# A graph layer and an 8-bit feed-forward layer on one core: where the 8-bit scale's factor is multiplied in, and the order of four steps around a maximum over all rows

## The chip, the cores and the metric

The kernel runs on one core of one Trainium2 chip. The metric is the device time of one execution in microseconds (us), as the median of several runs. Engines are named as the profile names them: PE is TensorE (PEld its weight load), DVE is VectorE, ACT is ScalarE, POOL is GpSimd, SP is SyncE, which here only issues transfers.

## What is computed

x is a 384 x 1024 matrix. A graph attention layer is added to it, then a feed-forward layer:

```python
x = x + gnn(layernorm(x))          # 16 heads, mask from 6528 edges
x = x + ffn(layernorm(x))

def act_fake_quant(x, clip):
    scale = sigmoid(clip) * max(abs(x)) / 127          # one number for the whole matrix
    return clip(round(x / scale), -128, 127) * scale

def ffn(x):                                            # w_*: quantised in the same way, one scale per row
    xq = act_fake_quant(x, clip_x)
    h = act_fake_quant(silu(xq @ w_gate.T) * (xq @ w_up.T), clip_down)    # 352 columns
    return h @ w_down.T
```

The two scales of act_fake_quant are what matters here. Each needs the largest absolute value of a whole matrix, so nothing of that matrix can be rounded before all of it is known.

## The kernel before

Rows are worked on in three tiles of 128 (t = 0, 1, 2), columns in blocks of 128 or halves of 512. The first 320 us compute the graph layer: projections (L189), scores, weights and products per pair of heads. The order on PE, SP and POOL is written out by hand for the whole kernel, and from L737 on that of DVE and ACT as well, so every engine works in the order of the program text, and an instruction that waits holds everything behind it on its engine. The 8-bit weights are quantised early. They lie in wgT, wuT and wdT, and their scales in w_scale and wd_scale.

The end of the kernel is what the change touches:

- *Last projection and residual* (L799 to L822). For each tile, matmuls (L814) go to PSUM, and `residual` (L746) adds x, takes the largest value (`hi`) along, makes the mean and variance statistics (L753) and the smallest value (`lo`, L754). Tile 2 is cut into groups of 512, 256, 128 and 128 columns, so that little is left to do after the last matmul.
- *`normalise`* (L756). It makes the mean and variance, and `far` (L770), the largest distance of a row from its mean, from `above` and `below`. The square root is on ACT (L764), and its reciprocal with one correction step (L773 to L779) gives `rstd`. `row_max` (L783) is far x rstd, taken together with the maximum of the earlier tiles: the largest absolute value that the row will have after normalisation, known without reading the row. Tiles 0 and 1 are normalised on ACT (L793, L794). Tile 2 is normalised on DVE, in two halves of 512 columns (L796).
- *Turning* (`turn`, L849). PE transposes the normalised tile into PSUM, eight 128 x 128 blocks (L855). Between the turns stand 14 or 17 transposes of the identity (`keep_busy`, L857, L861) that compute nothing.
- *The first scale* (L869). `all_max` (L127) spreads the column of row maxima over the partitions with one transpose (L129) and reduces it (L131), which gives the same largest value in every partition. `act_scale` (L835) multiplies it with sigmoid(clip) / 127 (L838), which is the scale sx, and takes the reciprocal rx (L840). sx goes to POOL, which makes the factors of the gate and up products (`gu_scale`, L873).
- *Conversion* (L881 to L886). There are six pieces of 128 x 512: three tiles by two halves of the columns. ACT multiplies those of tiles 0 and 1 with rx and writes int8 (L883), DVE those of tile 2 (L884). DVE casts all six from int8 to bf16 (L886).
- *Gate and up* (L888 to L911). Four column groups of 16 matmuls each (L895). Of the first 16, the first eight need the first half of the columns (three casts), the others the second half. ACT takes the sigmoid (L901), DVE makes the products (L903, L906) and the largest absolute value of each partition (L909), in a column of `hmx` for each group.
- *The second scale* (L918 to L922). 17 idle transposes, then DVE reduces hmx to one column (L920), and the same all_max and act_scale give sh and rh. h is converted (L929, L931) and cast (L934), multiplied with w_down (L943), scaled (L947), and added to x on POOL (L951, three pieces) and DVE (L955, three pieces). Each piece is then stored.

The factor sigmoid(clip) comes from L482, at about 31 us.

Of the kernel before, what the change touches and what calls it, by code (L numbers as in the profile page):

```python
# [23 lines left out]
F32 = mybir.dt.float32  # L24
# [3 lines left out]
AF = mybir.ActivationFunctionType  # L28
ALU = mybir.AluOpType
# [3 lines left out]
P = 128  # L33
# [28 lines left out]
def gnn_ffn_kernel(ctx: ExitStack, tc: tile.TileContext, a: dict, out: bass.AP):  # L62
# [74 lines left out]
    mask = ffn.tile([P, NT, N], F32)  # L137
    nc.gpsimd.memset(mask, NO_EDGE)
    sig = ffn.tile([P, 2], F32)

    ident_b = const.tile([P, P], BF16)
    later = ph1.tile([P, GROUP * P], F32, name="later", bufs=1)
# [94 lines left out]
    def run(steps):  # L237
        for _ in steps:
            pass
# [6 lines left out]
    with ph1_stack:  # L246
# [37 lines left out]
        def normalise(t, between=None):  # L284
            xn = rows_p.tile([P, F], F32, name="row")
            for j in range(2):
                hs = slice(j * 512, (j + 1) * 512)
                nc.vector.tensor_scalar(
                    xn[:, hs], x[:, t, hs], mv1[:, t, 0:1], rstd1[:, t : t + 1], op0=ALU.subtract, op1=ALU.mult
                )  # L290
            for g in range(2):
                pt = ps_tp.tile([P, 4, P], F32, name="tp")
                for j in range(4):
                    c = 4 * g + j
                    nc.tensor.transpose(pt[:, j, :], xn[:, c * P : (c + 1) * P], ident)
                nc.scalar.copy(xnT[:, 4 * g : 4 * g + 4, t * P : (t + 1) * P], pt)
                if g == 0 and between:
                    between()
# [156 lines left out]
        for i, (name, o) in enumerate(todo[:-1]):  # L455
            (wa, wb), sums = wq_next, sums_next
            right, dst, cols = work[name]

            if name == "wq" and o == FIRST:
                aside = tables()  # L460
            elif name == "wiq" and o == KC - 2:
                aside = k_steps
            else:
                aside = islice(groups, GROUP + 1)
            wq_next = [load_w(todo[i + 1][0], todo[i + 1][1] + j) for j in range(2)]
            sums_next, steps = left_sums(*wq_next, turned if todo[i + 1][0] == "wik" else ph1)
            if name == "wv" and o == KC - 4:
                q_right, q_steps = right_sums(qT, ph1, "right")
                work["wiq"] = (q_right, q2, bias_of(3))
            if name == "wv" and o >= KC - 4:  # L470
                steps = in_turn(steps, islice(q_steps, 4))
            if name == "wiq" and o == KC - 4:
                k_right, k_steps = right_sums(kT, turned, "k_right")
                steps = in_turn(steps, islice(k_steps, 4))
            aside = in_turn(aside, steps)
            run(project2(
                wa, wb, sums, right, dst[:, o], dst[:, o + 1], cols[:, o : o + 1], cols[:, o + 1 : o + 2], ps_p, "p",
                lambda: next(aside, None),
            ))
            run(aside)  # L480
            if i == 0:
                nc.scalar.activation(sig, clip, AF.Sigmoid)  # L482
        run(groups)


# [58 lines left out]
    with ExitStack() as ph:  # L544
# [211 lines left out]
        def normalise(t, last, st, hi, lo):  # L756

            mv = small.tile([P, 2], F32, name="mv2")
            nc.vector.bn_aggr(mv, st.rearrange("p a b -> p (a b)"))
            mean = mv[:, 0:1]  # L760
            var = small.tile([P, 1], F32, name="var2")
            nc.vector.tensor_scalar(var, mv[:, 1:2], EPS, None, op0=ALU.add)
            s0 = small.tile([P, 1], F32, name="s2")
            nc.scalar.activation(s0, var, AF.Sqrt)  # L764
            above = small.tile([P, 1], F32, name="above")
            nc.vector.tensor_scalar(above, hi[:, last : last + 1], hi[:, 0:1], mean, op0=ALU.max, op1=ALU.subtract)
            below = small.tile([P, 1], F32, name="below")
            nc.vector.tensor_scalar(below, lo[:, last : last + 1], lo[:, 0:1], mean, op0=ALU.min, op1=ALU.subtract)
            far = small.tile([P, 1], F32, name="far")
            nc.vector.tensor_scalar(far, below, -1.0, above, op0=ALU.mult, op1=ALU.max)  # L770

            r0 = small.tile([P, 1], F32, name="r2")
            nc.vector.reciprocal(r0, s0)  # L773
            vr = small.tile([P, 1], F32, name="vr2")
            nc.vector.tensor_scalar(vr, r0, var, r0, op0=ALU.mult, op1=ALU.mult)
            nw = small.tile([P, 1], F32, name="nw2")
            nc.vector.tensor_scalar(nw, vr, -0.5, 1.5, op0=ALU.mult, op1=ALU.add)
            rstd = small.tile([P, 1], F32, name="rstd2")
            nc.vector.tensor_mul(rstd, nw, r0)  # L779
            if t == 0:  # L780
                nc.vector.tensor_mul(row_max[:, 0:1], far, rstd)
            else:
                nc.vector.tensor_scalar(  # L783
                    row_max[:, t : t + 1], far, rstd, row_max[:, t - 1 : t], op0=ALU.mult, op1=ALU.max
                )
            if t < NT - 1:

                minus = small.tile([P, 1], F32, name="minus")
                nc.vector.tensor_scalar(minus, mean, -1.0, None, op0=ALU.mult)
            for g in range(2):  # L790
                gs = slice(g * 512, (g + 1) * 512)
                if t < NT - 1:
                    nc.scalar.activation(xn[:, t, gs], x[:, t, gs], AF.Identity, bias=minus)  # L793
                    nc.scalar.activation(xn[:, t, gs], xn[:, t, gs], AF.Copy, scale=rstd)  # L794
                else:
                    nc.vector.tensor_scalar(xn[:, t, gs], x[:, t, gs], mean, rstd, op0=ALU.subtract, op1=ALU.mult)  # L796


        for t in range(NT):  # L799
            if t < NT - 1:  # L800
                groups, part = [(0, 512), (512, 512)], 512
            else:
                groups, part = [(0, 512), (512, 256), (768, 128), (896, 128)], 128
            st = small.tile([P, F // part, 6], F32, name=f"st2_{part}")
            hi = small.tile([P, 4], F32, name="hi")
            lo = small.tile([P, 4], F32, name="lo")
            for g, (c0, width) in enumerate(groups):
                pm = open_groups.get((t, g)) if t < NT - 1 else None
                ks = [NP - 1]
                if pm is None:  # L810
                    pool, name = (ps_mm, "mm") if g < 2 else (ps_sc, "sc")
                    pm, ks = pool.tile([P, 512], F32, name=name), range(KC)
                for k in ks:
                    nc.tensor.matmul(  # L814
                        pm[:, :width], outT[:, k, t * P : (t + 1) * P], wo[k][:, c0 : c0 + width],
                        start=(k == 0), stop=(k == KC - 1),
                    )
                residual(t, g, c0, width, part, pm, st, hi, lo)
                if 0 < g < len(groups) - 1:
                    nc.vector.tensor_tensor(hi[:, 0:1], hi[:, 0:1], hi[:, g : g + 1], op=ALU.max)  # L820
                    nc.vector.tensor_tensor(lo[:, 0:1], lo[:, 0:1], lo[:, g : g + 1], op=ALU.min)
            normalise(t, len(groups) - 1, st, hi, lo)  # L822
        run(prep)


    with ExitStack() as ph:
# [5 lines left out]
        hmx = small.tile([P, 4], F32, name="hmx")  # L832
        nc.gpsimd.memset(hmx, 0.0)

        def act_scale(mx, which):  # L835

            s = small.tile([P, 1], F32, name=f"as{which}")
            nc.vector.tensor_scalar(s, mx, sig[:, which : which + 1], 1.0 / QMAX, op0=ALU.mult, op1=ALU.mult)  # L838
            r = small.tile([P, 1], F32, name=f"ar{which}")
            nc.vector.reciprocal(r, s)  # L840
            return s, r

# [21 lines left out]

        idle = small.tile([P, 1], F32, name="idle")
        nc.scalar.activation(idle, clip[:, 0:1], AF.Sigmoid)
        sx, rx = act_scale(all_max(row_max[:, NT - 1 : NT], pt[:, :P]), 0)  # L869
        turn(2)  # L870
        keep_busy(14, ps_x, "x")
        gu_scale = small.tile([P, 2, 3], F32, name="gu_scale")
# [8 lines left out]
        for g in range(2):  # L881
            for t in range(2):
                nc.scalar.activation(part(x8, t, g), xnT[t][g], AF.Copy, scale=rx)  # L883
            nc.vector.tensor_scalar(part(x8, 2, g), xnT[2][g], rx, None, op0=ALU.mult)  # L884
            for t in (0, 2, 1):
                nc.vector.tensor_copy(part(xqT, t, g), part(x8, t, g))  # L886

        for col, ic, c0, width in ((0, 0, 0, N), (1, 1, 0, N), (2, 2, 0, N // 2), (3, 2, N // 2, N // 2)):  # L888
# [28 lines left out]
            nc.scalar.copy(wd_scale_b[:, g * 512 : (g + 1) * 512], pt.rearrange("p a b -> p (a b)"))  # L917
        keep_busy(17, ps_x, "x")  # L918
        mx = small.tile([P, 1], F32, name="hmax")
        nc.vector.tensor_reduce(mx, hmx, axis=AX.X, op=ALU.max)  # L920
        pt = ps_tp.tile([P, P], F32, name="tp")
        sh, rh = act_scale(all_max(mx, pt), 1)  # L922

        h8 = ff.tile([P, 3, N], I8, name="h8", bufs=1)
        hq = ff.tile([P, 3, N], BF16, name="hq", bufs=1)
# [78 lines left out]
```

## Time and profile before

| what | value |
|---|---|
| median of 3 runs | 375.97 us (375.29 to 376.2) |
| the profiled execution's own time | 376.68 us |
| its span, first to last instruction | 374.9 us |
| mean granted PE clock | 0.994 |
| PE, DVE, ACT, POOL busy | 96%, 69%, 30%, 19% of the span |
| last matmul of the graph layer ends (L814) | 343.77 us |
| gate and up matmuls start (L895) | 350.28 us |
| conversion of h starts (L929) | 362.31 us |

All places in the text are us from the start of the span. The profile's page gives busy times by engine and the chain of work that ended last: followed back from the last instruction, at each step to what released it. The timeline lists instructions in order with start, length, engine, line and shape, and behind them in brackets how long the engine had idled and for whom. Lengths of neighbours on one engine overlap a little, since a step starts before the one ahead has left the pipeline. So the distance from start to start is what a step costs the engine, and start plus length is when its result is there. Each result that another instruction waits for is announced by a semaphore. A wait costs some hundredths of a us, even on the same engine.

### The profile page before, as it was taken

How to read it: one execution, taken by the hardware profiler on the slowest of the kernel's cores; microseconds unless marked ns; L12 is line 12 of the kernel's file. 1: busy time of each engine (PE TensorE's matmuls, PEld its weight loads, DVE VectorE, ACT ScalarE, POOL GpSimd, SP SyncE). 2: the span in 40 equal slices, each digit the busy share in tenths (PEclk: the TensorE clock that was granted, in tenths of full speed). 3: DMA queues.
4: the chain of work that ended last, by engine and by line, in shares of the span. 5: the costliest groups of instructions: out<-in, count | busy, mean ns of one | idle time of the engine just before them, and what ended most of it. 6: DMA issues, size and time to landing. Idle time of an engine off the chain costs nothing.

```text
span 374.9 us, 5872 instructions
## 1 busy us (share of the span) xinstructions
PE 358.8 (96%) x2113; PEld 298.9 (80%) x2113; DVE 260.2 (69%) x788; ACT 112.8 (30%) x264; POOL 72.1 (19%) x81
## 2 busy tenths in 40 slices
PE   8999999999999999799999999999999999999981
PEld 7899999999999999698877878686866545449660
DVE  5868888878889985998487457717492521199785
ACT  2152000100000000123672546446444523034330
POOL 6110254455444544210000000000000000000003
PEclk9999999999999999999999999999999999999997
DMA  8995433343333357148070040040294000000004
GB/s 236 393 376 213 150 114 112 116 133 114 112 112 115 112 170 247 57 119 289 21 231 32 19 129 23 18 171 1 101 375 132 31 0 2 0 0 3 1 0 168
DMA packets 17805, 44.50 MB, mean 119 GB/s; under 512 B 3263, under 2 KB 8401, under 8 KB 17393
## 3 DMA queue, kind: packets, MB, share of 16 engines
q1 hardware_dynamic: 15104, 39.46, 31.1%
q0 software_dynamic: 2672, 4.68, 4.2%
q8 instruction: 16, 0.26, 0.3%
q14 instruction: 13, 0.10, 0.1%
HBM read 41.91 MB, written 2.21 MB: 118 GB/s over the span
## 4 chain that ended last, share of the span: by engine, by line
PE 76%; DVE 12%; DMA 6%; ACT 3%; issue 1%; SPq 0%; DVEq 0%; ACTq 0%
PE p L189 34%; PE mm L580 7%; PE mm L189 6%; PE sc L641 4%; PE tp L633 4%; PE mm L651 3%; PE sc L651 3%; PE mm L814 3%; PE sc L603 3%; PE mm L303 3%; DMA row<-in_L_ffn_w_gate_dram 2%; DMA row<-in_L_ffn_w_down_dram 2%; DMA wt<-in_wik_dram 2%; PE sc L814 1%; DVE s L609 1%; DVE wmx L496 1%
## 5 line engine op out<-in xcount | busy, mean ns | idle before, releaser
L425 POOL DMA_INDIRECT mask_d<-value,place x51 | 56.9, 1115 | 66.3 <-DVE place L422 50.8
L189 PE MATMUL p<-actT,wt 128*128 128x192 f32 x360 | 65.9, 326 | 0.5 <-DVE actT L200 0.5
L189 PEld LDWEIGHTS p<-actT,wt 128*128 128x128 f32 x360 | 59.6, 190 | 0.8 <-DVE actT L200 0.8
L580 PE MATMUL mm<-wt,actT 128*128 128x256 f32 x192 | 46.1, 384 | 0.0
L580 PEld LDWEIGHTS mm<-wt,actT 128*128 128x128 f32 x192 | 34.8, 190 | 7.8 <-issue 2.2
L613 ACT ACTIVATE e<-s,mn 128x384 f32<-128x384 f32 x48 | 29.0, 605 | 26.4 <-DVE mn L609 26.4
L609 DVE CUSTOM_DVE_ANT_0 s<-sc,mask 128x384 f32<-128x384 f32 x48 | 24.5, 551 | 13.0 <-PE sc L603 12.8
L189 PE MATMUL p<-x_right,s 128*128 128x192 f32 x176 | 32.2, 326 | 0.0
L189 PE MATMUL p<-x_right,wt 128*128 128x192 f32 x176 | 32.2, 326 | 0.0
L831 POOL MEMSET hT<- 128x384 f32 x1 | 0.4, 418 | 156.9 <-PE sc L641 156.9
L189 PEld LDWEIGHTS p<-x_right,s 128*128 128x128 f32 x176 | 29.2, 190 | 0.0
L189 PEld LDWEIGHTS p<-x_right,wt 128*128 128x128 f32 x176 | 29.2, 190 | 0.0
L635 ACT COPY eTs<-tp 128x384 f32<-128x384 f32 x48 | 20.5, 478 | 25.3 <-PE tp L633 25.3
L412 DVE SCALAR_TENSOR_TENSOR junk<-key_b,key,later 128x384 f32<-128x384 f32 (+3 forms) x51 | 27.5, 539 | 0.0
L203 ACT COPY actT<-p 128x192 f32<-128x192 f32 x15 | 4.8, 319 | 66.9 <-PE p L189 66.9
L200 DVE SCALAR_TENSOR_TENSOR actT<-p,bias,actT 128x192 f32<-128x192 f32 x45 | 18.7, 415 | 8.5 <-PE p L189 6.6
L213 ACT ACTIVATE actT<-p,bias 128x192 f32<-128x192 f32 x15 | 6.3, 422 | 52.7 <-PE p L189 52.7
L633 PEld LDWEIGHTS tp<-ident,e 128*128 128x128 f32 x144 | 17.1, 140 | 4.9 <-issue 2.4
L633 PE MATMUL tp<-ident,e 128*128 128x128 f32 x144 | 19.7, 273 | 0.3 <-ACT eTs L635 0.3
L603 PE MATMUL sc<-k,actT 64*128 64x384 f32 x96 | 19.9, 518 | 0.0
L189 PE MATMUL mm<-actT,wt 128*128 128x192 f32 x96 | 18.9, 329 | 0.0
L496 DVE TENSOR_REDUCE wmx<-row 128x1 f32<-128x352 f32 (+2 forms) x14 | 11.4, 815 | 9.5 <-DMA row<-in_L_ffn_w_down_dram 6.4
(215 smaller groups left out, 596.3 us busy)
## 6 DMA issues: line engine op xcount, KB each, us to landing
wt<-in_wq_dram SPq DMA_DIRECT2D x8, 512.0 KB, 11.1
wt<-in_wk_dram SPq DMA_DIRECT2D x8, 512.0 KB, 4.3
wt<-in_wv_dram SPq DMA_DIRECT2D x8, 512.0 KB, 4.3
wt<-in_wiq_dram SPq DMA_DIRECT2D x8, 512.0 KB, 4.0
wt<-in_wik_dram SPq DMA_DIRECT2D x8, 512.0 KB, 4.5
wt<-in_wiv_dram SPq DMA_DIRECT2D x8, 512.0 KB, 5.3
wt<-in_wo_dram SPq DMA_DIRECT2D x8, 512.0 KB, 7.5
actT<-in_x_dram SPq DMA_DIRECT2D x6, 512.0 KB, 4.4
```

The costliest lines, as they stand in the source:

```text
L189: nc.tensor.matmul(z, left[:, k * P : (k + 1) * P], r[:, k, :], start=(k == 0), stop=(k == HK - 1))
L200: nc.vector.scalar_tensor_tensor(dst, z, b, with_, op0=ALU.add, op1=ALU.add)
L412: nc.vector.scalar_tensor_tensor(junk[:, :left], keys[:, (c - k0) * P : (c - k0) * P + left], key[:, c : c + 1], later[:, :left], op0=ALU. ...
L425: ins = nc.gpsimd.indirect_dma_start(out=mask_d, out_offset=bass.IndirectOffsetOnAxis(ap=place[:, c : c + 1], axis=0), in_=value[:, c : c ...
L496: nc.vector.tensor_reduce(mx[:rows], wn[:rows, :n], axis=AX.X, op=ALU.max, apply_absolute_value=True)
L580: nc.tensor.matmul(pm, vT[:, k, t * P : (t + 1) * P], wt[k // HK][:, k0 : k0 + 256], start=(k == 0), stop=(k == KC - 1),)
L603: nc.tensor.matmul(ps[t, h], q2[hs, t * P : (t + 1) * P], k2[hs, :], start=True, stop=True)
L609: nc.vector.tensor_tensor_reduce(s, ps[t, h], mask[:, t, :], -SCALE, 3.0e38, op0=ALU.add, op1=ALU.min, accum_out=mn[h][:, t : t + 1],)
L613: nc.scalar.activation(e[h][:, t, :], s, AF.Exp, bias=mn[h][:, t : t + 1], scale=-1.0, accum_out=sm[h][:, t : t + 1],)
L633: nc.tensor.transpose(pt[:, t * P : (t + 1) * P], e[h][:, t, m * P : (m + 1) * P], ident)
L635: nc.scalar.copy(eT[h][m], pt)
L651: nc.tensor.matmul(pm, outT[:, k, t * P : (t + 1) * P], wo[k][:, gs], start=(k == 0), stop=(k == KC - 1))
```

## The change

sigmoid(clip) / 127 is no longer multiplied onto the maximum over all partitions, but onto what goes into it. A new tile `per_max` holds the factor: column 0 for the first scale, columns 1 to 4 for the second. ACT makes it behind L482. In `normalise` the old `far` is now called `size`, and `far` is size x per_max, in all three tiles. For the second scale, the reduction of hmx becomes a multiplication with a maximum in one DVE instruction, which gives the column by an accumulator. What all_max returns is then the scale itself, and only the reciprocal is left to do.

The two halves of tile 2's normalisation leave `normalise`: the first stands ahead of the reduction of all_max on DVE, the second behind the reciprocal. On PE nothing is moved: the transposes of tile 2 still stand behind that of all_max, four for each half, and 14 idle ones follow.

Of the six conversions the last (tile 2, second half) goes from DVE to ACT, where it is the fifth. The casts of the first half now begin with tile 2, those of the second half end with it. In the built program the order on PE, POOL and SP is as it was; ACT has three instructions more, DVE one more: three more `far`, one accumulator read, less the two multiplications of act_scale and the one conversion.

```diff
+    per_max = ffn.tile([P, 5], F32)
...
                 nc.scalar.activation(sig, clip, AF.Sigmoid)
+                nc.scalar.activation(per_max[:, 0:1], sig[:, 0:1], AF.Copy, scale=1.0 / QMAX)
+                nc.scalar.activation(
+                    per_max[:, 1:5], sig[:, 1:2].to_broadcast([P, 4]), AF.Copy, scale=1.0 / QMAX
+                )
...
+            size = small.tile([P, 1], F32, name="size")
+            nc.vector.tensor_scalar(size, below, -1.0, above, op0=ALU.mult, op1=ALU.max)
             far = small.tile([P, 1], F32, name="far")
-            nc.vector.tensor_scalar(far, below, -1.0, above, op0=ALU.mult, op1=ALU.max)
+            nc.vector.tensor_mul(far, size, per_max[:, 0:1])
...
-                else:
-                    nc.vector.tensor_scalar(xn[:, t, gs], x[:, t, gs], mean, rstd, op0=ALU.subtract, op1=ALU.mult)
+            return mean, rstd
...
-        def act_scale(mx, which):
-
-            s = small.tile([P, 1], F32, name=f"as{which}")
-            nc.vector.tensor_scalar(s, mx, sig[:, which : which + 1], 1.0 / QMAX, op0=ALU.mult, op1=ALU.mult)
-            r = small.tile([P, 1], F32, name=f"ar{which}")
-            nc.vector.reciprocal(r, s)
-            return s, r
+        def last_tile(g):
+            gs = slice(g * 512, (g + 1) * 512)
+            t = NT - 1
+            nc.vector.tensor_scalar(xn[:, t, gs], x[:, t, gs], mean, rstd, op0=ALU.subtract, op1=ALU.mult)
...
-        sx, rx = act_scale(all_max(row_max[:, NT - 1 : NT], pt[:, :P]), 0)
+        last_tile(0)
+        sx = all_max(row_max[:, NT - 1 : NT], pt[:, :P])
+        rx = small.tile([P, 1], F32, name="ar0")
+        nc.vector.reciprocal(rx, sx)
+        last_tile(1)
         turn(2)
...
-            nc.vector.tensor_scalar(part(x8, 2, g), xnT[2][g], rx, None, op0=ALU.mult)
-            for t in (0, 2, 1):
+            if g == 0:
+                nc.vector.tensor_scalar(part(x8, 2, g), xnT[2][g], rx, None, op0=ALU.mult)
+            else:
+                nc.scalar.activation(part(x8, 2, g), xnT[2][g], AF.Copy, scale=rx)
+            for t in ((2, 0, 1), (0, 1, 2))[g]:
                 nc.vector.tensor_copy(part(xqT, t, g), part(x8, t, g))
...
-        nc.vector.tensor_reduce(mx, hmx, axis=AX.X, op=ALU.max)
+        scaled = small.tile([P, 4], F32, name="hscaled")
+        nc.vector.tensor_tensor_reduce(
+            scaled, hmx, per_max[:, 1:5], 1.0, -3.0e38, op0=ALU.mult, op1=ALU.max, accum_out=mx
+        )
...
-        sh, rh = act_scale(all_max(mx, pt), 1)
+        sh = all_max(mx, pt)
+        rh = small.tile([P, 1], F32, name="ar1")
+        nc.vector.reciprocal(rh, sh)
```

More of the change, by code (lines that the diff above doesn't have):

```diff
@@ L789, in normalise @@
                 nc.vector.tensor_scalar(minus, mean, -1.0, None, op0=ALU.mult)
-            for g in range(2):
-                gs = slice(g * 512, (g + 1) * 512)
-                if t < NT - 1:
+                for g in range(2):
+                    gs = slice(g * 512, (g + 1) * 512)
                     nc.scalar.activation(xn[:, t, gs], x[:, t, gs], AF.Identity, bias=minus)
                     nc.scalar.activation(xn[:, t, gs], xn[:, t, gs], AF.Copy, scale=rstd)
-                else:
-                    nc.vector.tensor_scalar(xn[:, t, gs], x[:, t, gs], mean, rstd, op0=ALU.subtract, op1=ALU.mult)
+            return mean, rstd
         for t in range(NT):
@@ L821, in gnn_ffn_kernel @@
                     nc.vector.tensor_tensor(lo[:, 0:1], lo[:, 0:1], lo[:, g : g + 1], op=ALU.min)
-            normalise(t, len(groups) - 1, st, hi, lo)
+            mean, rstd = normalise(t, len(groups) - 1, st, hi, lo)
         run(prep)
@@ L833, in gnn_ffn_kernel @@
         nc.gpsimd.memset(hmx, 0.0)
-        def act_scale(mx, which):
-            s = small.tile([P, 1], F32, name=f"as{which}")
-            nc.vector.tensor_scalar(s, mx, sig[:, which : which + 1], 1.0 / QMAX, op0=ALU.mult, op1=ALU.mult)
-            r = small.tile([P, 1], F32, name=f"ar{which}")
-            nc.vector.reciprocal(r, s)
-            return s, r
+        def last_tile(g):
+            gs = slice(g * 512, (g + 1) * 512)
+            t = NT - 1
+            nc.vector.tensor_scalar(xn[:, t, gs], x[:, t, gs], mean, rstd, op0=ALU.subtract, op1=ALU.mult)
         pt = ps_x.tile([P, 512], F32, name="x")
```

## The prediction

> **What bounds the kernel now.** I first read the page's busy shares and its chain that ended last. TensorE is busy for 96% of the span and carries 76% of the chain, so anything that only lightens VectorE in the first 320 us moves nothing.
>
> ```profile
> PE 76%; DVE 12%; DMA 6%; ACT 3%; issue 1%; SPq 0%; DVEq 0%; ACTq 0%
> ```
>
> Part of VectorE's 12% lies at the end, where one number (the largest value of all rows) must be known before anything can be rounded to 8 bits. The chain in order of time (start, us, what) shows that piece: row maximum, first normalised half, eight transposes of the last tile, conversion to int8, casts, matmuls.
>
> ```profile
> 345.47 0.21 DVE far L770
> 345.69 0.08 DVE r L773
> ...
> 346.76 0.46 DVE actT L796
> ...
> 347.27 1.12 PE mm L855 x8
> ...
> 348.42 0.75 DVE x L884
> 349.17 1.06 DVE xqT L886 x3
> 350.23 0.66 DVE x L884
> 350.89 1.01 DVE xqT L886 x3
> ...
> 351.94 0.32 PE mm L895
> ```
>
> The timeline (start, us, engine, line) of the same stretch corrects one step of it.
>
> ```profile
> 346.87 0.27 PE L129 MATMUL x<-ident,row_max 128*128 128x128 f32 x1
> ...
> 347.58 0.28 DVE L131 TENSOR_REDUCE allmax<-x 128x1 f32<-128x128 f32 x1
> 347.90 0.21 DVE L838 TENSOR_SCALAR as<-allmax,sig 128x1 f32<-128x1 f32 x1
> 348.15 0.16 DVE L840 RECIPROCAL ar<-as 128x1 f32<-128x1 f32 x1
> 348.21 1.69 PE L861 MATMUL x<-ident 128*128 128x128 f32 x14
> 348.22 0.32 POOL L873 TENSOR_SCALAR gu_scale<-w_scale,as 128x6 f32<-128x6 f32 x1 [27.44 <-DVE as L838]
> 348.41 0.69 ACT L883 ACTIVATE x<-tp,ar 128x512 int8<-128x512 f32 x1 [1.58 <-PE mm L855]
> ```
>
> The chain releases L884 by the eight transposes (348.39). But L884 waits for only the fourth of them, and ScalarE's L883, which reads transposes that were done near 345, starts at the same moment. What releases both is the reciprocal L840, which ends at 348.15 + 0.16 = 348.31; the two waits of each cost the other 0.10. And the reciprocal is late for two reasons: L131 could have started at 347.18 (L129 ends at 347.14), but stood at 347.58 behind both halves of L796; and L838 lies between.
>
> **The change, step by step** (times on the old axis).
>
> *One more VectorE step before the maximum* (far becomes size, then far), once per tile. The old L770 to L773 distance is 0.14 (345.47 to 345.61). Now size takes 0.21 and 0.03 of wait, and far lets the reciprocal start about 0.08 later (as 332.97 to 333.05 behind a row_max product): 0.32, so +0.18. Bounds: +0.08 if the wait is hidden, +0.30 if the reciprocal waits for the whole of far (0.16). I take 0.18; the same two-step spacing stands all over this chain. In tiles 0 and 1 it adds 2 x 0.18 = 0.36 to a VectorE run that is unbroken from 327.33 to 343.47. There it is covered by the wait for the last matmul of tile 2:
>
> ```profile
> 343.80 0.29 DVE L748 CUSTOM_DVE_ANT_0 actT<-sc,actT 128x128 f32<-128x128 f32 x1 [0.33 <-PE sc L814]
> ```
>
> That is 0.33, and 0.41 counted from where the next step could be issued (343.39). So 0 here; without that cover 0.36.
>
> *Maximum and reciprocal.* Row maximum ends at 346.76 + 0.18 = 346.94, the first half runs 346.86 to 347.40, L129 ends at 347.32, L131 runs 347.36 to 347.64 (no second half before it), the reciprocal 347.68 to 347.84 (no L838 before it). Old end 348.31: 0.47 earlier. ScalarE starts its conversions at 347.94.
>
> *The second half moves behind the reciprocal.* It starts about 0.08 after it does, at 347.76, and ends at 348.30 (0.54 each), instead of 347.67. Behind it on VectorE stands the conversion of tile 2, first half: it starts at about 348.27 (old 348.42) and ends at 349.02; three casts at 0.34 pitch then end at 350.18 (old 350.23). Behind it on TensorE's queue stand four transposes, 14 filler transposes (L861) and then gate/up. Transposes from 348.35 at 0.1175 (eight took 347.27 to 348.21) reach 348.82; fillers at 0.109 ((1.69 - 0.27)/13) free the queue at 350.35. Gate/up therefore starts at 350.35, held by the fillers, not at 350.23 when its data are there; before it was 350.28.
>
> *Fifth conversion on ScalarE.* Its five pieces at 0.575 pitch (348.41, 348.99, 349.56, 350.13 before) start at 347.94 to 350.24; the last ends at 350.93. VectorE loses one 0.66 step, so the last cast runs 350.96 to 351.38. The first eight gate/up matmuls take 1.31 (350.28 to 351.59), so the ninth is due at 350.35 + 1.31 = 351.66, and its data are there at 351.43. Before it stood at 351.94, after a gap. **Gain 0.28**; from there TensorE has the same work.
>
> *Second scale.* The chain between the last fillers and the quantisation of h:
>
> ```profile
> 360.90 0.16 DVE L920 TENSOR_REDUCE hmax<-hmx 128x1 f32<-128x4 f32 x1
> 361.21 0.29 PE L129 MATMUL tp<-ident,hmax 128*128 128x128 f32 x1
> 361.54 0.29 DVE L131 TENSOR_REDUCE allmax<-tp 128x1 f32<-128x128 f32 x1 [0.48 <-PE tp L129]
> 361.87 0.21 DVE L838 TENSOR_SCALAR as<-allmax,sig 128x1 f32<-128x1 f32 x1
> 362.12 0.16 DVE L840 RECIPROCAL ar<-as 128x1 f32<-128x1 f32 x1
> ```
>
> L838 goes: 362.12 - 361.87 = **0.25 gained**. The plain reduction becomes a custom reduction with an accumulator read. Its rows are 0.68 for 512 columns and 0.284 for 128 from PSUM, or 1.03 ns a column, hence some 0.16 for 4. Bounds: 0 more than L920, or as long as the whole 128-column pair (343.80 to 344.13, 0.33 against 0.16: 0.17 more); 0.07 of that is covered, as the fillers leave TensorE free only for 361.18. So 0 to 0.10; I take 0.03, near the row's slope.
>
> *Two small ScalarE steps at 31 us* (0.20 each by L482): ScalarE idles for 3.26 before its next copy at 34.38. Nothing; 0.4 if that cover went.
>
> **Sum**: -0.28 - 0.25 + 0.03 = -0.50 us. The profiled execution took 376.68 (span 374.9 and 1.78 around it); it stands 0.71 above the median of 375.97. Its own time would become 376.18, the median 375.47, which I give as 375.5, 0.13% less. About 0.3% (1.1 us) is what a measurement of this kernel can tell from no change, so I call this "same".
>
> **A rule against it.** The row first: at the end POOL's L951 and VectorE's L955, both SBUF additions, run together, and the first L955 takes 1.14 where the others take 0.68.
>
> ```profile
> 365.01 3.71 POOL L951 TENSOR_TENSOR y<-actT,y 128x512 f32<-128x512 f32 x3 [16.47 <-DVE y L947]
> ...
> 368.14 1.14 DVE L955 TENSOR_TENSOR y<-actT,y 128x512 f32<-128x512 f32 x1
> ```
>
> The Trainium skill ("SBUF — State Buffer", section "Who interferes with whom") says that VectorE and GpSimd share one port pair as an exclusive lock: a VectorE instruction in a two-port mode, tensor_scalar among the candidates, or a GpSimd one, whichever starts first, blocks the other for its whole length. By that rule the sum is -0.50 if the second half wins and about -0.18 if gu_scale does; by the plain durations it is -0.50.
>
> **The rivals.**
> *gu_scale stands in the way.* It started 0.11 after L838's end; now it starts 0.11 after L131, at 347.75, within 0.01 of the second half. Before, no wide SBUF step of VectorE lay there. If the half waits for gu_scale's 0.32, transposes, fillers and gate/up move by 0.32: sum -0.18, 375.8. For it: the L955 row. Against: the start is a dead heat, and 6 columns need little.
>
> *The moved half costs more than it frees (slower).* Place: second half, then four transposes, then fillers, in TensorE's order. It decides from a second half that ends 0.50 later than worked out (after 348.80). The price from the row: if the half is stretched as L955 was, to 1.14, it ends 0.60 later, and the sum is +0.10: 376.1. Against: POOL's L951 lasted much longer than gu_scale.
>
> *More than worked out.* The extra step costs 0.08 rather than 0.18, and gate/up starts with its data at 350.23 rather than behind the fillers: -0.50 - 0.10 - 0.12 = -0.72, or 375.25. Against: fillers are in order.
>
> *It doesn't shorten anything*: if L884 did wait for all eight transposes, as the chain has it, it would start at about 349.0 instead of 348.42, and the first casts end at 350.85. Gate/up would start at 350.90, the ninth matmul at 352.21, 0.27 later than before: sum +0.27 - 0.25 + 0.03 = +0.05, 376.0. Against: it waits for the fourth.
>
> **How the numbers follow.** Forecast 0.50 (375.5); gu_scale in the way 0.22 (375.8); more than worked out 0.12 (375.25); slower 0.10 (376.1); no gain 0.06 (376.0). The three runs spread by 0.9, so a median can lie some 0.4 off. Range: 375.25 - 0.45 = 374.8 to 376.1 + 0.2 = 376.3. A gain of over 0.3% (below 374.84) needs the best cases and a low median: 0.15. Over 0.3% slower (above 377.1) needs the slower rival, and twice its price again: 0.05. Within: 0.80.
>
> **What would show it.** L131's successor starting 0.04 after L129's end instead of 0.44; the reciprocal's end 0.4 to 0.5 earlier; no gap in TensorE between the eighth and ninth gate/up matmul; fillers ending against gate/up; reciprocal straight behind the second L131. Wrong would be: the second half starting at gu_scale's end, a gap ahead of gate/up's ninth matmul, a custom reduction well over 0.2, or VectorE late for tile 2's last residual (the 0.33 wait gone).

## The result and the profile after

The changed kernel takes 375.55 us (median of 14 runs, 374.89 to 376.39), the kernel before 376.04 in as many runs beside it (375.2 to 377.33). The ratio is 0.9987 with a 95% interval of 0.9974 to 0.9999: 0.49 us or 0.13% less, at the edge of what the measurement can tell. The profiled execution has a span of 374.6 us.

The runs of one kernel spread by 1.5 to 3.3 us, so the steps are better compared inside a profile. Most of the spread comes from the first 340 us: the last 32 matmuls of the last projection (L814, after the change L820) start anywhere from 338.56 to 341.32 in the thirteen profiles of this study. From there to the conversion of h the engines repeat themselves to hundredths. This distance, **D**, is the yardstick below. There is one profile of each kernel; how well D repeats can be told from e6 and e11 below, which add only a GpSimd step to the changed kernel and both give 21.80, against its 21.79. Before it is 362.31 - 340.02 = 22.29 us, after 361.73 - 339.94 = 21.79. What follows h is alike: from there to the end of the span 12.56 to 12.66 in twelve of them, and 12.87 in the one shown here, which is why its span fell by less than D.

The chain by engine still has TensorE at 76%:

```profile
PE 76%; DVE 13%; DMA 5%; ACT 2%; POOL 1%; issue 1%; DVEq 0%; SPq 0%; POOLq 0%; ACTq 0%
```

VectorE around the first scale (timeline after; start, us, engine, line, shape):

```profile
345.39 0.21 DVE L776 TENSOR_SCALAR size<-below,above 128x1 f32<-128x1 f32 x1
345.64 0.16 DVE L778 TENSOR_TENSOR far<-size,per_max 128x1 f32<-128x1 f32 x1
345.71 0.15 DVE L781 RECIPROCAL r<-s 128x1 f32<-128x1 f32 x1
...
346.79 0.54 DVE L844 TENSOR_SCALAR actT<-actT,mv,rstd 128x512 f32<-128x512 f32 x1
347.29 0.29 DVE L131 TENSOR_REDUCE allmax<-x 128x1 f32<-128x128 f32 x1
347.61 0.16 DVE L875 RECIPROCAL ar<-allmax 128x1 f32<-128x1 f32 x1
347.69 0.53 DVE L844 TENSOR_SCALAR actT<-actT,mv,rstd 128x512 f32<-128x512 f32 x1
348.14 0.74 DVE L892 TENSOR_SCALAR x<-mm,ar 128x512 int8<-128x512 f32 x1
348.92 1.83 DVE L896 CAST xqT<-x 128x512 bf16<-128x512 int8 x5
350.90 0.43 DVE L896 CAST xqT<-x 128x512 bf16<-128x512 int8 x1 [0.15 <-ACT x L894]
```

The last group starts 0.08 earlier on this axis, so 0.08 is to be added before a place is held against one of before. The reciprocal ends at 347.77 (347.85 on the old axis, 348.31 before). The reduction L131 starts 0.04 after its transpose (346.93 + 0.32 = 347.25) and no longer behind the second half. Five casts run without a gap, and only the last waits, 0.15, for ScalarE's fifth conversion, which ends at 350.87. GpSimd's gu_scale starts 0.01 ahead of the second half:

```profile
347.68 0.58 POOL L880 TENSOR_SCALAR gu_scale<-w_scale,allmax 128x6 f32<-128x6 f32 x1 [26.98 <-DVE allmax L131]
...
350.17 0.70 ACT L894 ACTIVATE x<-mm,ar 128x512 int8<-128x512 f32 x1
```

TensorE in the same stretch:

```profile
348.28 0.66 PE L858 MATMUL mm<-ident,actT 128*128 128x128 f32 x4 [0.24 <-DVE actT L844]
348.77 1.69 PE L864 MATMUL x<-ident 128*128 128x128 f32 x14
350.30 0.33 PE L905 MATMUL mm<-xqT,wgT 128*128 128x384 bf16 x1
...
351.44 0.33 PE L905 MATMUL x<-xqT,wuT 128*128 128x384 bf16 x1
351.60 0.33 PE L905 MATMUL mm<-xqT,wgT 128*128 128x384 bf16 x1
```

The transposes of the second half now wait for the moved half, the 14 fillers follow, and gate/up starts straight behind them. The ninth matmul (351.60) follows the eighth at the pace of the others; the gap of before is closed.

The second scale, VectorE alone:

```profile
360.56 0.16 DVE L931 CUSTOM_DVE_ANT_0 hscaled<-hmx,per_max 128x4 f32<-128x4 f32 x1
360.64 0.08 DVE L931 DVE_READ_ACCUMULATOR2_ANT hmax<- 128x1 f32 x1
361.21 0.29 DVE L131 TENSOR_REDUCE allmax<-tp 128x1 f32<-128x128 f32 x1 [0.48 <-PE tp L129]
361.53 0.16 DVE L937 RECIPROCAL ar<-allmax 128x1 f32<-128x1 f32 x1
361.73 0.48 DVE L944 TENSOR_SCALAR h<-hT,ar 128x384 int8<-128x384 f32 x1
```

The custom reduction takes 0.16 like the plain one, its accumulator read lies inside it, and the reciprocal stands straight behind the maximum.

### The profile page after: what moved, and what is told of

The parts are those of the page before. It is cut to its first block, busy times and chain, and to the rows that moved or that the text cites. A ratio compares the mean times of both kernels' runs of the same rounds, so it can differ in the third digit from the quotient of the medians.

```text
span 374.6 us, 5875 instructions
## 1 busy us (share of the span) xinstructions
PE 359.1 (96%) x2112; PEld 300.1 (80%) x2113; DVE 260.0 (69%) x789; ACT 113.6 (30%) x267; POOL 72.9 (19%) x81
## 4 chain that ended last, share of the span: by engine, by line
PE 76%; DVE 13%; DMA 5%; ACT 2%; POOL 1%; issue 1%; DVEq 0%; SPq 0%; POOLq 0%; ACTq 0%
PE p L190 34%; PE mm L190 9%; PE mm L586 8%; PE sc L609 4%; PE tp L639 4%; PE sc L647 4%; PE mm L657 3%; PE sc L657 3%; DMA edges_i<-in_edge_type_dram 2%; DMA row<-in_L_ffn_w_gate_dram 2%; PE mm L304 2%; DVE st L759 1%; DMA row<-in_L_ffn_w_down_dram 1%; DVE y L962 1%; DVE e L629 1%; PE mm L905 1%
## 5 line engine op out<-in xcount | busy, mean ns | idle before, releaser
L629 DVE TENSOR_SCALAR e<-e,rs 128x384 f32<-128x384 f32 x48 | 17.2, 416 | 0.4
```

Of the source, the lines that this page charges most:

```text
L629: nc.vector.tensor_scalar(e[h][:, t, :], e[h][:, t, :], rs[:, t : t + 1], None, op0=ALU.mult)
```

## The experiments

The theory is that of the prediction: two gains one behind the other on the chain, 0.26 at the ninth gate/up matmul and 0.24 at the second scale, less an extra step of 0.18 that the first has already paid. The main rival is that the moved half, GpSimd or the fillers set the first gain. In the table, D is measured inside each profile.

| run | what differs | D expected | D measured |
|---|---|---|---|
| before / after | | | 22.29 / 21.79 |
| e1 | before, second scale alone | 22.04 | 22.06 |
| e2 | after, both halves together | 21.97 | 21.98 |
| e3 | after, fifth conversion on VectorE | 22.01 | 21.93 |
| e4 | after, 10 fillers for 14 | 21.59 | 21.57 |
| e5 | after, factor in the identity | 21.63 | 21.91 |
| e6 | after, a GpSimd step beside the half | 22.1 to 22.7 | 21.80 |
| e7 | e5 with 12 and 10 fillers | 21.41 | 21.70 |
| e8 | after, two more steps in tiles 0 and 1 | 22.5 | 22.52 |
| e9 | after, far behind the reciprocal | 21.63 | 21.61 |
| e10 | e9 with 12 and 10 fillers | 21.4 | 21.38 |
| e11 | after, e6's step released later | 21.8 | 21.80 |

**e1, the second scale alone.** The kernel before with `per_max`, the multiplying reduction of hmx, and the reciprocal straight behind all_max.

> The kernel before, with the second scale's part of the change alone (factor multiplied in with the reduction of hmx; first scale, halves and conversions as before). Yardstick for all runs: D, the distance inside one profile from the start of the last 32 matmuls of the last projection to the start of VectorE's conversion of h; it is 22.29 us before and 21.79 after. My theory: the two parts of the gain lie one behind the other on the chain and are independent, so D = 22.29 - 0.25 = 22.04, with the custom reduction hidden behind the 17 fillers. Rival (the second part only pays because the first came earlier): D = 22.29.

D fell by 0.23. The second part pays without the first; the other 0.27 of the 0.50 belongs to the first scale.

**e2, the two halves together again.**

```diff
         last_tile(0)
+        last_tile(1)
         sx = all_max(row_max[:, NT - 1 : NT], pt[:, :P])
...
         nc.vector.reciprocal(rx, sx)
-        last_tile(1)
```

> The changed kernel with both halves of tile 2's normalisation ahead of the reduction of the maximum again. Theory: the reduction then starts at 347.69 instead of 347.29 (0.90 of issue for two halves), the reciprocal and ScalarE's five conversions 0.40 later, the last cast ends near 351.73, so the ninth gate/up matmul starts 0.18 later and with a gap ahead of it: D = 21.79 + 0.18 = 21.97. The fillers end earlier (near 349.9), so gate/up itself starts at its casts, near 350.2. Rival (the half was moved for nothing, since the fillers hold gate/up anyway): D = 21.79 or less.

D grew by 0.19. Gate/up started 10.29 after the last group (350.49 - 340.20; after: 350.30 - 339.94 = 10.36), so earlier, and the ninth matmul later, at 11.85 instead of 11.66, behind a gap. The eighth and the ninth, which in the kernel after stand 0.16 apart:

```profile
351.64 0.33 PE L905 MATMUL x<-xqT,wuT 128*128 128x384 bf16 x1
352.05 0.32 PE L905 MATMUL mm<-xqT,wgT 128*128 128x384 bf16 x1
```

**e3, the fifth conversion back on VectorE.** The branch for g = 1 removed, its casts in the order 0, 2, 1.

> The changed kernel with the sixth conversion back on VectorE (and its cast order 0, 2, 1 in the second half). Theory: VectorE converts from 350.0 to 350.75 and then casts until 351.77, so the ninth gate/up matmul comes 0.22 later, with a gap of 0.2 ahead of it: D = 22.01. Rival (VectorE is not what the ninth matmul waits for, the fillers are): D = 21.79.

```profile
350.01 0.74 DVE L891 TENSOR_SCALAR x<-mm,ar 128x512 int8<-128x512 f32 x1
350.67 1.09 DVE L893 CAST xqT<-x 128x512 bf16<-128x512 int8 x3
```

VectorE ends at 351.76 and the ninth matmul starts at 351.81: VectorE is what it waits for, but D grew by 0.14, not by 0.22. The rest is the expectation's place for the conversion. This run's last group starts 0.07 later than that of the kernel after (340.01 against 339.94), so 350.0 means 350.07 here and the casts' end 351.84; the conversion started 0.06 and the casts ended 0.08 earlier than that. Without ScalarE's help and the new cast order of the second half the change is worth 0.36 instead of 0.50.

**e4, ten fillers.** `keep_busy(14, ps_x, "x")` behind `turn(2)` becomes `keep_busy(10, ...)`.

> The changed kernel with 10 instead of 14 filler transposes ahead of gate/up. Theory: the fillers hold gate/up (its data are there at about 350.1, the queue is free at 350.30), so gate/up starts 0.2 earlier, the ninth matmul at 351.40 just behind its cast (351.38): D = 21.59, and 0.2 us less in the time, near 375.35 if the kernel after stands at 375.55. Rival (gate/up is held by the casts, as before the change): D = 21.79, with a gap of 0.43 between the last filler and gate/up.

```profile
348.39 1.26 PE L864 MATMUL x<-ident 128*128 128x128 f32 x10
349.69 0.10 PEld L905 LDWEIGHTS <-wgT 128*128 128x128 bf16 x1 [0.28 <-DVE xqT L896]
349.69 0.34 PE L905 MATMUL mm<-xqT,wgT 128*128 128x384 bf16 x1
```

D fell by 0.22, the whole of it ahead of gate/up (349.69 - 339.56 = 10.13, after 10.36). The fillers did hold it. Four of them take 0.43 (1.69 against 1.26), but only half of that is gained: with ten, gate/up's first weight load (PEld) waits for the third cast, so the casts hold it again and taking out more fillers should bring nothing (not tried). The time is 375.16 us (12 runs) against 376.08 of the kernel before on the same chip, ratio 0.9973 (0.9955 to 0.9990).

**e5, the factor in the identity.** `far` and the reduction of hmx as before the change; all_max multiplies by a scaled identity instead:

```diff
-        nc.tensor.transpose(ps_tile, col.to_broadcast([P, P]), ident)
+        nc.tensor.matmul(ps_tile, col.to_broadcast([P, P]), ident_f[:, j, :], start=True, stop=True)
```

> The changed kernel with the factor in neither far nor the reduction of hmx: the spreading of the maximum over the partitions is a matmul with an identity that was multiplied by sigmoid(clip)/127 at 31 us. VectorE loses the extra step in all tiles and the custom reduction becomes the plain one again. Theory: the extra step costs 0.18 on the chain of tile 2; the spreading can come only 0.14 earlier, as the first 14 fillers end then, and everything behind it moves by 0.14 to 0.18: D = 21.63, with a wait of VectorE of about 0.33 for the last group of tile 2 again. Rival (the extra step was hidden by the square root or by the fillers): D = 21.79.

A miss. TensorE around the second scale:

```profile
360.02 0.46 PE L129 MATMUL tp<-ident_f,hmax 128*128 128x128 f32 x2
```

What was one instruction of 0.29 as a transpose is two as a matmul in float32, 0.46 together, and 0.43 instead of 0.32 at the first scale. VectorE did lose the step: it waited 0.32 for the last group again, and the spreading began 0.14 earlier (345.98 - 339.13 = 6.85, after 6.99). But the longer spreading took most of that back (the reduction L131 began 7.31 behind the last group instead of 7.35), and 0.16 more came in at the second scale (ninth matmul to h: 10.29 instead of 10.13). The time is 376.11 us, ratio to before 1.0009 (0.9987 to 1.0031). So this run could not say what the extra step costs.

**e6, a GpSimd step beside the second half.**

```diff
+        aside = ff.tile([P, 512], F32, name="aside", bufs=1)
+        nc.gpsimd.tensor_scalar(aside, x[:, 0, :512], row_max[:, NT - 1 : NT], None, op0=ALU.mult)
         last_tile(0)
```

> The changed kernel with one more GpSimd step, a 128x512 multiplication from x into a tile that nobody reads, released by the row maximum, so that it is running when VectorE's second half is due. Theory of a shared access that only one of the two engines has at a time: the half waits for the end of that step or is stretched, by 0.3 to 0.9 us, and D grows by as much (22.1 to 22.7), while the half takes over 0.8 instead of 0.53 or starts late. Rival (the two engines do not hold each other up, and gu_scale's 0.58 instead of 0.32 has another reason): the half stays at 0.53 and D at 21.79.

The second miss, and one that settles the rival. GpSimd, then VectorE:

```profile
345.60 1.80 POOL L873 TENSOR_SCALAR aside<-actT,row_max 128x512 f32<-128x512 f32 x1 [26.28 <-DVE row_max L791]
```

```profile
346.24 0.16 DVE L877 RECIPROCAL ar<-allmax 128x1 f32<-128x1 f32 x1
346.32 0.53 DVE L844 TENSOR_SCALAR actT<-actT,mv,rstd 128x512 f32<-128x512 f32 x1
346.76 0.74 DVE L894 TENSOR_SCALAR x<-mm,ar 128x512 int8<-128x512 f32 x1
```

By the profile, whose spans of GpSimd are rough, it was at work from 0.72 before the half began to 0.55 after it ended, and the half took its 0.53 behind the reciprocal as ever. D did not move (21.80). GpSimd does not hold up this VectorE step.

**e11, the same step by itself.** Released by a one-column copy of the last cast's result, when VectorE is idle.

> The changed kernel with the same extra 128x512 GpSimd step as the run with one ahead of the second half, but now released by the last cast, when VectorE is idle for some 2 us. It measures the step by itself; it took 1.80 beside VectorE's two halves. Theory: VectorE's steps with one tensor are not held up by GpSimd, but hold it up, by about their own length, as with gu_scale (0.58 instead of 0.32): the step takes 0.5 to 0.8 less when alone, 1.0 to 1.3. Rival (no engine holds the other, the step takes 1.80 in itself): 1.80. D stays at 21.8 in both.

```profile
351.20 1.57 POOL L901 TENSOR_SCALAR aside<-actT,row_max 128x512 f32<-128x512 f32 x1
```

Alone 1.57, beside VectorE's halves 1.80: 0.23 more, of the size of gu_scale's 0.58 against 0.32, but well below what I had expected (1.0 to 1.3 alone). Both readings were off; GpSimd is the one that loses, and a little. In e6 it began 0.19 into the first half (345.41) and ran through the whole second one; which of the two cost it the 0.23 isn't shown.

**e8, two more steps in tiles 0 and 1.** Two dependent multiplications of far by 1 for t < 2.

> The changed kernel with two more dependent one-column VectorE steps (a multiplication by 1 each) behind far in tiles 0 and 1 only, four in all at some 0.19. Theory: the 0.33 us that VectorE waited for the last group of tile 2 before the change is used up by the change (VectorE now goes from step to step without a wait there), so every further step arrives on the chain: D = 21.79 + 0.7 = 22.5. Rival (the cover is still there, or something else hides tiles 0 and 1): D = 21.79 to 22.2.

D grew by 0.73: nothing is left of the cover. The line of the kernel after says the same, for it has no wait any more where 0.33 stood before:

```profile
343.71 0.29 DVE L754 CUSTOM_DVE_ANT_0 actT<-sc,actT 128x128 f32<-128x128 f32 x1
```

**e9, far behind the reciprocal.** The two lines that make `far` stand behind the two that make `r0`.

> The changed kernel with far = size x per_max emitted behind the reciprocal of the square root instead of ahead of it, in all tiles. Nothing else differs. Theory: the extra step costs 0.18 only because it stands in front of the reciprocal, which doesn't need it; behind it, it fits into the wait from the reciprocal to vr. The row maximum is then known 0.13 to 0.18 earlier, VectorE waits again for the last group of tile 2 (some 0.3), and D goes from 21.79 to 21.63 (limited by the first 14 fillers, which end 0.14 ahead of the spreading of the maximum). Rival (the scaled identity showed no gain because the extra step was free): D = 21.79.

```profile
345.88 0.21 DVE L776 TENSOR_SCALAR size<-below,above 128x1 f32<-128x1 f32 x1
346.01 0.15 DVE L778 RECIPROCAL r<-s 128x1 f32<-128x1 f32 x1
346.13 0.16 DVE L780 TENSOR_TENSOR far<-size,per_max 128x1 f32<-128x1 f32 x1
346.20 0.27 DVE L782 TENSOR_SCALAR vr<-r,var 128x1 f32<-128x1 f32 x1
```

From size to reciprocal 0.13 instead of 0.32, and vr stands where it would without the extra step. D fell by 0.18. This settles what e5 left open: the extra step did cost its 0.18.

**e7 and e10, combinations.** e5 and e9, each with 12 instead of 14 fillers ahead of the maximum and 10 instead of 14 ahead of gate/up. The first expectation is that of e7, the second that of e10 ("the same" is e9).

> The scaled identity together with 12 instead of 14 fillers ahead of the maximum and 10 instead of 14 ahead of gate/up. Theory: the gains add, 0.18 and 0.2: D = 21.41, and 0.4 us less than the kernel after (near 375.15). Rival (one of the two is taken back by the other, since gate/up is then held by the casts): D = 21.55 to 21.6.

> The same, with 12 instead of 14 fillers ahead of the maximum and 10 instead of 14 ahead of gate/up. Theory: the gains add, 0.18 + 0.22: D = 21.4, some 0.4 below the kernel after in the time (near 375.15 if that stands at 375.55), and the best of all versions. Rival: D = 21.57, as with ten fillers alone.

e7: D 21.70 instead of 21.41, off by what e5 was off, and within 0.01 of e5's 21.91 less e4's 0.22; ratio to before 0.9982 (0.9963 to 1.0002). e10: D 21.38, 0.41 below the changed kernel and 0.91 below the one before, the best by D. Its time is 375.47 us against 376.45 beside it, ratio 0.9974 (0.9955 to 0.9992). By time alone it can't be told from e4. The 12 fillers bring next to nothing in either: in e10 the spreading begins 0.06 earlier than in e9 but takes 0.32 instead of 0.27, and the reduction L131 starts at 7.15 behind the last group instead of 7.16. So the gain over the changed kernel is that of e9 and of e4.

## Why the prediction was right

It gave 375.5 for the measured 375.55, as the sum -0.50 from two terms of 0.28 and 0.25 and a cost of 0.03. That the time came within 0.05 is partly luck: by the prediction's own account a median can lie some 0.4 off. What the profiles bear out is the sum and where it comes from: D fell by 0.50, with 0.26 where 0.28 was worked out and 0.24 where it was 0.22. Step by step, on the old axis:

- *One more step before the maximum, +0.18.* Size to reciprocal is 0.32 after the change against 0.14, as worked out; e9 gets it back. *Its cover in tiles 0 and 1*: right, but with nothing to spare. The cost of 0.36 was set against a cover of 0.41; no wait is left, and e8 shows that the next step there counts in full. The prediction had named the lost wait as a sign of being wrong, with VectorE late for the last residual. The wait is gone, but VectorE is not late: 343.71 + 0.08 = 343.79, before 343.80.
- *Maximum and reciprocal.* Reciprocal's end 347.85 (expected 347.84), first conversion on ScalarE 347.95 (347.94). e2 shows the position of the second half to be worth 0.19. What leaving out L838 is worth here by itself was not tried. An estimate from the spacings: it saves 0.25 (347.90 to 348.15) and the extra step takes 0.18 of it back, so moving the factor nets some 0.07 at the first scale, and the order of the steps and the fifth conversion do the rest.
- *The second half moves behind the reciprocal.* It ended at 348.30 as expected, gate/up started at 350.38 (350.35), held by the fillers, as e4 shows.
- *Fifth conversion on ScalarE, gain 0.28.* 0.26 measured (351.94 to 351.68). That the ninth matmul would else wait for VectorE is shown by e3, with 0.14 (the expectation had 0.22).
- *Second scale, -0.25 + 0.03.* From the ninth matmul to h it is 10.13 instead of 10.37, so -0.24, and e1 alone has -0.23. The custom reduction cost nothing: it ended at 360.72, and the fillers let the transpose start only at 360.87.
- *gu_scale in the way* (chance 0.22). The dead heat came as worked out, 347.68 against 347.69, but the half was not held. Its price came from an unlike row: L955 beside L951 adds two tensors from SBUF, while the half reads one. In all thirteen profiles the first of these additions takes 1.14 to 1.16 while GpSimd still adds, and the two behind it 0.68; e6 shows that the half is not held. GpSimd's steps differ as well (L951 adds two tensors, e6's step multiplies one), so that the number of tensors decides is likely but not shown. The Trainium skill ("SBUF — State Buffer", section "Who interferes with whom") lets whichever starts first block the other for its whole length if VectorE's step is in a two-port mode. In e6 GpSimd began 0.72 ahead and the half took its 0.53 all the same, so either the half is in no such mode or the rule doesn't hold for this pair. No run shows the mode. An estimate from the kernel before speaks for the second: a step of the half's form takes 0.27 on one column (L766) and 0.54 on 512 (L796), some 0.53 ns a column, where a two-tensor step with 0.16 (L821) and 0.68 (L955) needs 1.01. The half runs at about twice the pace, as two columns at a time would.
- *More than worked out*: not seen. The extra step cost 0.18 and not 0.08, and gate/up started behind the fillers.
- *The moved half costs more than it frees*, and *it doesn't shorten anything*: not seen. The half ended 0.50 ahead of the point from which the first would decide. L892 started at 348.22 on the old axis while the eighth transpose ended at 349.02 (348.28 + 0.66 + 0.08), so it does wait for the fourth only. (The second rival's own sum is some 0.06 short: from the forecast's start of 348.27, a start at 349.0 puts the casts' end at 350.91 and not 350.85. It changes nothing.)

## What to carry to other kernels

Where a chain of small steps ends a kernel, a step that is put in ahead of another that doesn't need it costs its full spacing; the same step behind it, in the wait for that one's result, costs nothing (0.18 against 0 here). When a step moves earlier, look at what stood beside it for cover: fillers that were cut to the old wait become the bound (0.22 here), and a wait of 0.33 that hid other work is gone after one use. And where runs spread more than the change is worth, measure inside the profile, from a point ahead of the change to one behind it.

## What the runs showed of the hardware

- Spreading a column over the partitions took one instruction of 0.27 to 0.32 us as a transpose and two of 0.43 to 0.49 together as a float32 matmul with a scaled identity (e5, e7).
- A one-tensor VectorE step of 512 columns (the half) took 0.53 to 0.54 with GpSimd idle or busy on SBUF (e6). A two-tensor one (L955 and its like) took 1.14 to 1.16 beside GpSimd's addition and 0.68 without, in all thirteen profiles. GpSimd's 128x512 step took 1.57 alone (e11) and 1.80 beside two halves (e6), its 128x6 step (gu_scale) 0.31 to 0.32, or 0.58 beside a half. Why GpSimd loses 0.23 to 0.26 is open, and its spans are rough.
- A reduction with an accumulator read costs no more than a plain one at 4 columns (0.16 each); the read of 0.08 lies within it (both end at 360.72).
